# The front of the first expert layer in finer steps: three sequences by turns, inverse roots from logarithm and exponential, router products two token tiles at a time

## The chip, the cores and the metric

The kernel runs on one core of a Trainium2 chip, as one program. The metric is the device time of one execution in microseconds (us); the kernel before took 5645.84 us as the median of 3 runs (5634.86 to 5657.25). The engines are named as in the profile: PE is the matrix engine (TensorE; PEld is its weight load, which overlaps PE), DVE is VectorE, ACT is ScalarE, POOL is GpSimd, SP is the engine whose queue issues most of the DMAs.

## The reference

The network is two layers on x of shape (8, 1024, 256) in float32: eight sequences of 1024 tokens with 256 channels. Layer 0 is an expert layer, causal attention, and the same expert layer again; layer 1 is a channel mix, a state-space block and a channel mix. Every block works on the layer norm of x and is added to x. What matters here is the start of the first expert layer, which this document calls the front:

```python
def _layernorm(x, axis=-1, eps=1e-05):
    m = jnp.mean(x, axis=axis, keepdims=True)
    v = jnp.var(x, axis=axis, keepdims=True)
    return (x - m) / jnp.sqrt(v + eps)

# in _L0_ffn_ref, on xf = the layer norm of x, 8192 rows of 256
logits = xf @ Wr + br                 # 8 experts
Sm = jax.nn.softmax(logits, axis=-1)
G_t, idx_t = jax.lax.top_k(Sm.T, k)   # k = 8192 / 8 = 1024 tokens for each expert
...
x = x + 0.5 * _L0_ffn_ref(_layernorm(x, axis=-1), ...)
x = x + _L0_attn_ref(_layernorm(x, axis=-1), ...)
x = x + 0.5 * _L0_ffn_ref(_layernorm(x, axis=-1), ...)
```

For every token the front makes the normalised row, the eight logits and their softmax.

## The kernel before, in words

A sequence lies in on-chip memory as a tile `xt` of 128 partitions by 8 token tiles by 256 channels. `tile_macaron_kernel` loads all eight sequences by eight DMAs, runs the front over them, then picks the tokens of each expert (`moe.chosen`, which calls `choose`), then runs the experts (`moe.run`), then attention, then layer 1. `choose` needs the probabilities of all eight sequences, so the end of the front is a point that everything behind waits for.

The front is a Python generator, `Moe.steps_front`, whose `yield`s cut it into steps. The loop in `tile_macaron_kernel` holds up to two of these generators and gives each a step by turns; a new one may enter at every fourth turn. Inside `tc.manual_schedule()` each engine gets its instructions in the order in which the program issues them, so the turns fix every engine's queue; each engine works through its queue in that order and waits where an input is missing.

The steps of one sequence in `Moe.steps_front` are: `net.normalise` as one step (the statistics of the 8 token tiles, L75 and L77 on DVE; the square root on ACT, L79; the reciprocal on DVE, L81; eight subtract-and-scale operations on DVE, L88); then four steps with the transposes of two token tiles each (L180 on PE, 4 transposes; L184 copies the PSUM bank to `moe_xT` on ACT); then one step with all router products (L189: 16 matmuls in float32, which the trace shows as 32 records) and the addition of the bias (L194 on DVE); then the softmax, in which L203 is the exponential on ACT; then the write of the rows (`rows`, SP's queue) and of the probabilities (`S`, L213). After a sequence the loop writes `xt` to `acc` on SP's queue. The square root and the exponential are in different table sets of ACT, so a load of a table stands ahead of some of them.

The class `Attention` has its own version of the front, `Attention.steps_front`, which the kernel already uses for the second expert layer, one sequence at a time within attention (`store` calls it). It goes in finer steps: `Attention.stats` takes two token tiles a step, and gets the inverse root from ACT's logarithm and exponential (L619, L620) and one Newton step of four small POOL operations (L623 to L626), with one POOL operation ahead (L615). Two token tiles are normalised in one step (L876) and transposed in the next (L683, through `transposed`). The router products go two token tiles at a time (L890: 4 matmuls, 8 records), each pair with its own PSUM bank and its own bias addition (L894). Banks come from `bank`, and what empties a bank is held back in the object `Pipe` until the next bank is asked for, by whichever sequence asks.

Of the kernel before, what the change touches and what calls it, by code (L numbers as in the profile page):

```python
# [14 lines left out]
PSUM = bass.MemoryType.PSUM  # L15
# [1734 lines left out]
@with_exitstack  # L1750
def kernel(
    ctx: ExitStack,
    tc: tile.TileContext,
    x: bass.AP,
    w_qkv: bass.AP,
    w_out: bass.AP,
    b_out: bass.AP,
    Wr: bass.AP,
    br: bass.AP,
    W_up: bass.AP,  # L1760
    b_up: bass.AP,
    W_down: bass.AP,
    b_down: bass.AP,
    ln_gamma: bass.AP,
    ln_beta: bass.AP,
    in_proj_t: bass.AP,
    conv_w: bass.AP,
    conv_b: bass.AP,
    x_proj_t: bass.AP,
    dt_proj_t: bass.AP,  # L1770
    dt_proj_b: bass.AP,
    A_log: bass.AP,
    Dp: bass.AP,
    out_proj_t: bass.AP,
    Wr_t: bass.AP,
    Wk_t: bass.AP,
    Wv_t: bass.AP,
    mu_r: bass.AP,
    mu_k: bass.AP,
    out: bass.AP,  # L1780
):
    nc = tc.nc
    B, T, _ = x.shape
    net = Net(ctx, tc, B, T)
    N, NT = net.N, net.NT

    of_moe = ctx.enter_context(ExitStack())
    mcp = of_moe.enter_context(tc.tile_pool(name="moe", bufs=1, side="right"))
    moe = Moe(mcp, net, Wr, br, W_up, b_up, W_down, b_down)
    S = moe.probabilities(mcp)  # L1790
    dram1 = ctx.enter_context(tc.tile_pool(name="dram1", bufs=1, space=DRAM))
    dram2 = ctx.enter_context(tc.tile_pool(name="dram2", bufs=2, space=DRAM))

    acc = [dram1.tile([N, D], F32, name=f"acc{i}") for i in range(2)]
    rows = [dram1.tile([N, ROW], F32, name=f"rows{i}") for i in range(2)]

    def of(a, b):

        return a[b * T : (b + 1) * T, :].rearrange("(c p) d -> p c d", p=P)

    def pool_in(st, name, bufs, **kw):
        return st.enter_context(tc.tile_pool(name=name, bufs=bufs, **kw))

    xf, of_out = x.rearrange("b t d -> (b t) d"), out.rearrange("b t d -> (b t) d")
    with ExitStack() as st:
        at = Attention(net, pool_in(st, "at_w", 1), w_qkv, w_out, b_out)
        with ExitStack() as ro:
            room = moe.room(ro)
            with ExitStack() as ph, tc.manual_schedule():
                pool, px = pool_in(ph, "f", 2), pool_in(ph, "f_x", B)  # L1810
                ps = pool_in(ph, "f_ps", 3, space=PSUM)
                xs = []
                for b in range(B):
                    xs.append(px.tile([P, NT, D], F32, name="xt"))
                    nc.sync.dma_start(xs[b], of(xf, b))

                todo, works = list(range(B)), []
                turn = 0
                while todo or works:
                    if todo and len(works) < 2 and turn % 4 == 0:  # L1820
                        b = todo.pop(0)
                        works.append((b, moe.steps_front(pool, ps, xs[b], b, rows[0], S, "mm")))
                    turn += 1
                    for b, steps in list(works):
                        if next(steps, 0) == 0:
                            works.remove((b, steps))
                            nc.sync.dma_start(of(acc[0], b), xs[b])
            with tc.manual_schedule():
                moe.chosen(S, room)
        with tc.manual_schedule():  # L1830
            moe.run(S, rows[0], acc[0])
        with ExitStack() as ph:
            at.places(pool_in(ph, "at_qk", 1), dram1)
            pools = {
                name: pool_in(ph, f"at_{name}", bufs) for name, bufs in (
                    ("x", 3), ("xn", 2), ("xT", 1), ("side", 1), ("pT", 4), ("so", 2), ("oT", 2),
                    ("over", 2), ("sm", 2), ("junk", 1), ("r", 1), ("rT", 1),
                )
            }
            for name, banks in (("s1", 3), ("s2", 3), ("po", 1), ("mm", 1)):  # L1840
                pools[name] = pool_in(ph, f"at_{name}", banks, space=PSUM)

            pools["dram"] = dram2

            def load(xt, b):
                nc.sync.dma_start(xt, of(acc[0], b))

            def store(xt, b):
                nc.sync.dma_start(of(acc[1], b), xt)
                yield from at.steps_front(moe, xt, b, rows[1], S)  # L1850

            with tc.manual_schedule():
                at.run(pools, load, store)
    with ExitStack() as st:
        w = pool_in(st, "l1_w", 1)
        layer1 = Layer1(
            net, w, Wr_t, Wk_t, Wv_t, mu_r, mu_k, ln_gamma, ln_beta, in_proj_t, conv_w, conv_b,
            x_proj_t, dt_proj_t, dt_proj_b, A_log, Dp, out_proj_t,
        )
        with tc.manual_schedule():  # L1860
            with ExitStack() as ro:
                moe.chosen(S, moe.room(ro))
            moe.run(S, rows[1], acc[1])
        of_moe.close()
        pools = {
            name: pool_in(st, f"l1_{name}", bufs) for name, bufs in (
                ("x", 2), ("mixT", 1), ("ka", 2), ("r", 2), ("hT", 2), ("u", 1), ("uc", 2 * NDC),
                ("xd", 1), ("delta", 1), ("du", 1), ("sp1", 1), ("zs", 1),
                ("rep", 1), ("sdl", 3), ("sdu", 3), ("dbu", 2), ("hc", 6), ("tap", 1), ("through", 1), ("xn", 2), ("small", 2),
            )  # L1870
        }
        pools["dram"] = dram2
        pools["ps"] = pool_in(st, "l1_ps", 2, space=PSUM)
        pools["y"] = pool_in(st, "l1_y", 1, space=PSUM)
        pools["h"] = pool_in(st, "l1_h", 2, space=PSUM)

        def load(xt, b):
            nc.sync.dma_start(xt, of(acc[1], b))

        def store(xt, b):  # L1880
            nc.sync.dma_start(of(of_out, b), xt)

        def load_x(xt, b):
            nc.sync.dma_start(xt, of(acc[0], b))

        def keep_x(xt, b):
            nc.sync.dma_start(of(acc[0], b), xt)

        with tc.manual_schedule():
            layer1.run(pools, load, load_x, keep_x, store)  # L1890
# [39 lines left out]
```

## Time and profile before

| what | us |
|---|---|
| median of 3 runs (lowest, highest) | 5645.84 (5634.86, 5657.25) |
| the profiled execution's own time | 5638.44 |
| its span, first to last instruction | 5636.2 |
| start of the first statistics, end of the last copy to `S` | 12.20, 109.25 |
| `choose` and the list of the first experts behind it, to where PE fills up again | about 109 to 210 |
| mean granted clock of PE over the span | 0.888 |

The profile counts an engine as busy while it executes an instruction. "Idle before, releaser" gives the idle time of an engine ahead of an instruction, and what ended it. The clock column gives what share of the full clock PE was granted in a stretch. [...] Most of the front's stage lies in the first of the 40 slices of the page, so the stage is read from stretches cut by hand.

### The profile page before, as it was taken

The numbers are of one execution on the slowest core, as the hardware profiler recorded it, in microseconds if no ns is written. First come the engines' busy times: TensorE is split into PE (matmuls) and PEld (weight loads), VectorE is DVE, ScalarE is ACT, GpSimd is POOL, SyncE is SP. The second block draws the span as 40 slices with busy tenths as digits, with TensorE's granted clock in tenths as the row PEclk, the third lists the DMA queues.
The fourth block names the chain that finished last, engine by engine and source line by source line (L and its number), as shares of the span: only waits on it lengthen the run. The fifth ranks groups of instructions, "written<-read, shape, count | busy, mean of one in ns | idle before, by whom it ended". The sixth has DMA issues, their size and how long they took to land.

```text
span 5636.2 us, 60291 instructions
## 1 busy us (share of the span) xinstructions
PE 4643.4 (82%) x21302; PEld 2203.4 (39%) x21302; DVE 3432.4 (61%) x5653; ACT 2503.6 (44%) x4150; POOL 2204.0 (39%) x1801
## 2 busy tenths in 40 slices
PE   5699699999999997499776778787787878878767
PEld 5365334444444442265433233332333324333324
DVE  5532166667766672533108877777767677677884
ACT  2111155655556653011135546465564655646443
POOL 1234111111111110234317656556556565556662
PEclk6799789999999997599888889889898888989888
DMA  6132212212222221122215554535445463454642
GB/s 209 32 64 53 73 45 77 67 63 77 74 67 65 74 69 47 48 55 58 41 40 141 145 141 111 155 107 149 126 109 156 112 160 109 113 150 119 168 136 64
DMA packets 252976, 545.28 MB, mean 97 GB/s; under 512 B 29681, under 2 KB 143681, under 8 KB 252674
## 3 DMA queue, kind: packets, MB, share of 16 engines
q1 hardware_dynamic: 228098, 507.34, 32.0%
q0 software_dynamic: 24576, 34.10, 3.7%
q8 instruction: 168, 2.75, 0.2%
q14 instruction: 134, 1.10, 0.1%
HBM read 400.31 MB, written 141.03 MB: 96 GB/s over the span
## 4 chain that ended last, share of the span: by engine, by line
PE 26%; DVE 13%; ACT 6%; issue 5%; DMA 2%; POOL 1%; SPq 0%; DVEq 0%; POOLq 0%; ACTq 0%
DVE h L1729 8%; PE y L1657 5%; PE pc L1376 4%; PE pr L1271 4%; PE pk L1249 4%; PE pu L1427 2%; DVE hc L1734 2%; PE pp L1511 2%; ACT h L1635 2%; PE pd L1442 1%; PE pm L472 1%; ACT xn L1205 1%; PE px L1406 1%; DMA sdu<-du 1%; PE po L489 1%
## 5 line engine op out<-in xcount | busy, mean ns | idle before, releaser
L777 ACT ACTIVATE pT<-s 128x512 f32<-128x512 f32 (+3 forms) x1536 | 670.8, 488 | 554.4 <-PE s L734 545.0
L1635 ACT ACTIVATE h<-sdl,A 128x1024 f32<-128x1024 f32 x512 | 567.0, 1112 | 645.4 <-DVE hc L1734 623.7
L734 PE MATMUL s<-kT,qT 32*128 32x512 f32 (+3 forms) x3072 | 841.6, 541 | 12.6 <-DVE mx L750 7.9
L1657 PE MATMUL y<-hc,pick 128*32 128x512 f32 x2048 | 654.7, 720 | 227.7 <-DVE hc L1734 227.7
L734 PE MATMUL s<-qT,kT 32*128 32x512 f32 (+3 forms) x3072 | 763.8, 548 | 13.1 <-ACT pT L777 13.1
L1626 POOL TENSOR_TENSOR dbu<-sdu,b 128x1024 f32<-128x1024 f32 x256 | 602.2, 2352 | 407.3 <-DMA sdu<-du 209.7
L1729 DVE TENSOR_TENSOR_SCAN h<-h,dbu 128x1024 f32<-128x1024 f32 x256 | 586.1, 2289 | 185.6 <-ACT h L1635 159.7
L1729 DVE TENSOR_TENSOR_SCAN h<-h,sdu 128x1024 f32<-128x1024 f32 x256 | 586.1, 2290 | 158.1 <-ACT h L1635 140.7
L1734 DVE TENSOR_TENSOR hc<-h,c 128x1024 f32<-128x1024 f32 x512 | 625.3, 1221 | 32.2 <-PE y L1657 3.4
L783 POOL TENSOR_SCALAR_AFFINE_SELECT pT<-pT 128x512 f32<-128x512 f32 x256 | 162.4, 634 | 1180.2 <-ACT pT L777 1095.0
L1626 POOL TENSOR_TENSOR sdu<-sdu,b 128x1024 f32<-128x1024 f32 x256 | 602.4, 2353 | 15.3 <-DMA b<-bc 4.7
L734 PEld LDWEIGHTS s<-kT,qT 32*128 32x128 f32 x3072 | 327.0, 187 | 438.9 <-DVE mx L750 186.7
L476 ACT ACTIVATE mid<-pm,bu 128x512 f32<-128x512 f32 x192 | 131.6, 686 | 722.2 <-PE pm L472 722.2
L747 DVE TENSOR_REDUCE part<-s 128x1 f32<-128x512 f32 x512 | 329.5, 685 | 186.5 <-PE s L734 185.9
L1657 PEld LDWEIGHTS y<-hc,pick 128*32 128x32 f32 x2048 | 127.0, 125 | 717.4 <-issue 395.2
L497 POOL DMA_INDIRECT acc<-o,idx x128 | 208.5, 1629 | 492.6 <-DVE o L494 228.0
L750 DVE CUSTOM_DVE_ANT_0 junk<-s,mask,part 128x256 f32<-128x256 f32 (+3 forms) x512 | 281.5, 550 | 160.0 <-PE s L734 115.2
L472 PE MATMUL pm<-tT,wu 128*128 128x512 f32 x768 | 364.4, 612 | 0.0
L489 PE MATMUL po<-wd,mid 128*128 128x256 f32 x1536 | 346.1, 388 | 0.0
L797 PE MATMUL po<-pT,at_v 128*32 128x512 f32 (+3 forms) x3072 | 337.2, 512 | 0.3 <-POOL pT L783 0.3
L750 DVE CUSTOM_DVE_ANT_0 junk<-s,mask 128x256 f32<-128x256 f32 (+3 forms) x512 | 250.2, 489 | 142.7 <-PE s L734 90.1
L489 PEld LDWEIGHTS po<-wd,mid 128*128 128x128 f32 x1536 | 300.0, 196 | 43.3 <-issue 1.0
(262 smaller groups left out, 6696.1 us busy)
## 6 DMA issues: line engine op xcount, KB each, us to landing
sdl<-dl SPq DMA_DIRECT2D x256, 512.0 KB
sdu<-du SPq DMA_DIRECT2D x256, 512.0 KB
acc<-xt SPq DMA_DIRECT2D x24, 1024.0 KB
xt<-acc SPq DMA_DIRECT2D x24, 1024.0 KB
rows<-moe_r SPq DMA_DIRECT2D x16, 1056.0 KB
qT<-padded_q SPq DMA_DIRECT2D x32, 512.0 KB
kT<-padded_k SPq DMA_DIRECT2D x32, 512.0 KB
kept<-so SPq DMA_DIRECT2D x64, 256.0 KB
```

The lines of the kernel that those rows point to most:

```text
L472: nc.tensor.matmul(pm, wu[:, k, n * P : (n + 1) * P], tT[:, k, t0 : t0 + HALF], start=(k == 0), stop=(k == KC - 1),)
L489: nc.tensor.matmul(po, mid[:, n, j * P : (j + 1) * P], wd[:, n, :], start=(n == 0), stop=(n == NF - 1),)
L734: self.net.nc.tensor.matmul(s[:, 0 : rhs.shape[-1]], lhsT, rhs, start=True, stop=True)
L747: nc.vector.tensor_reduce(part, sh, AX.X, ALU.max)
L750: nc.vector.tensor_tensor_reduce(junk[:, 0:w], sh[:, 0:w], self.mask[:, W - w : W], 1.0, part if a else -3e38, ALU.add, ALU.max, self.mx[n ...
L777: self.net.nc.scalar.activation(pT[:, h, 0:w], sh[:, 0:w], AF.Exp, scale=1.0 / HD**0.5)
L797: nc.tensor.matmul(q.po[h * HS : (h + 1) * HS, o:W], self.va[q.b % 2][:, j, g * HG + h, :], pT[:, h, 0 : W - o], start=(j == 0), stop=(j = ...
L1626: nc.gpsimd.tensor_tensor(inputs[i], t, seqs[b].rep["b", p], ALU.mult)
L1635: nc.scalar.activation(decays[i], spread["dl", i - p], AF.Exp, scale=self.A[:, p, n : n + 1])
L1657: nc.tensor.matmul(self.py[g * self.RG : (g + 1) * self.RG, t0 : t0 + W], self.pick[:, j, :], hc[:, t0 : t0 + W], start=False, stop=(j == ...
L1729: nc.vector.tensor_tensor_scan(decays[i], decays[i], inputs.pop(i), 0.0, ALU.mult, ALU.add)
L1734: nc.vector.tensor_tensor(hc, decays.pop(i), seqs[b].rep["c", p], ALU.mult)
```

## The change

The loop in `tile_macaron_kernel` takes the generator from `Attention.steps_front` in place of the one from `Moe.steps_front`. It holds up to three sequences, and one may enter at every ninth turn. The pools are those that the new generator asks for: four buffers of each small tile, three of the row tile and of the transposed tile, four PSUM banks. ACT's table set with both the logarithm and the exponential is loaded once, ahead of the loop. The functions called (`Attention.stats`, `transposed`, `steps_front`, `bank`, `Pipe`) are unchanged, and nothing behind the loop is changed.

```diff
             with ExitStack() as ph, tc.manual_schedule():
-                pool, px = pool_in(ph, "f", 2), pool_in(ph, "f_x", B)
-                ps = pool_in(ph, "f_ps", 3, space=PSUM)
+                px = pool_in(ph, "f_x", B)
+                at.pools = {
+                    name: pool_in(ph, f"f_{name}", bufs) for name, bufs in (
+                        ("sm", 4), ("r", 3), ("rT", 3),
+                    )
+                }
+                at.pools["mm"] = pool_in(ph, "f_mm", 4, space=PSUM)
+                at.pipe = at.Pipe()
+                nc.scalar.preload_act_table_set("natural_log_exp_and_others")
                 xs = []
...
-                    if todo and len(works) < 2 and turn % 4 == 0:
+                    if todo and len(works) < 3 and turn % 9 == 0:
                         b = todo.pop(0)
-                        works.append((b, moe.steps_front(pool, ps, xs[b], b, rows[0], S, "mm")))
+                        works.append((b, at.steps_front(moe, xs[b], b, rows[0], S)))
```

The called generators, as they stand:

```python
def stats(self, x, got):                 # L600-627
    for c0 in range(0, NT, 2):
        yield ""
        for c in range(c0, c0 + 2):
            nc.vector.bn_stats(st[:, c, :], x[:, c, :])
        for c in range(c0, c0 + 2):
            nc.vector.bn_aggr(mv[:, c, :], st[:, c, :])
    yield ""
    nc.gpsimd.tensor_scalar(v, mv[:, :, 1], 1e-5, None, ALU.add)
    yield ""
    nc.scalar.activation(r, v, AF.Ln)
    nc.scalar.activation(r, r, AF.Exp, scale=-0.5)
    yield ""
    ...                                  # four POOL operations

def steps_front(self, moe, x, b, rows, S):   # L862-920
    yield from self.stats(x, got)
    for c0 in range(0, NT, 2):
        yield ""
        ...                              # L876, two token tiles
        yield "pe"
        self.transposed(r, c0, ...)      # 4 transposes, copy held back in Pipe
    for c0 in range(0, NT, 2):
        yield "pe"
        pl = self.bank([P, 2, E], "pl")
        ...                              # L890, 4 matmuls
        self.pipe.filled(...)            # L894, bias, held back in Pipe
    yield ""
    self.pipe.flush()
    ...                                  # maximum, difference
    yield ""
    nc.scalar.activation(lg, lg, AF.Exp)
    yield ""
    ...                                  # sum, reciprocal, product
    yield ""
    ...                                  # copy to S, DMA of the rows
```

## The prediction

> **What bounds the kernel now.** I read the page first. Its line of granted clocks begins at 6 tenths, so the first slice, where the change lies, is one in which PE is throttled. Then I cut the front's stage by pairs of sequences and read the busy time of the engines (columns: length, PE, PEld, DVE, ACT and POOL busy with instruction counts, PE's clock, DMA share, GB/s):
>
> ```profile
> 12.20:35.19 22.99, 15.05 (x96) 14.44 (x96) 15.01 (x65) 8.06 (x14) 0.00 (x0) 0.85 1.10 348
> 35.19:57.77 22.58, 14.75 (x96) 13.93 (x96) 15.00 (x65) 8.05 (x14) 0.00 (x0) 0.65 0.62 213
> 57.77:86.58 28.81, 20.96 (x96) 20.14 (x96) 15.11 (x66) 8.05 (x14) 0.00 (x0) 0.50 0.50 165
> 86.58:109.37 22.79, 14.75 (x96) 13.93 (x97) 15.09 (x65) 8.05 (x14) 0.00 (x0) 0.65 0.51 170
> ```
>
> The stage is 97 us, 1.7% of the span. A pair takes 22.6 to 28.8 us and keeps DVE busy 15 of them, so no engine is full; the clock decides between 22.8 and 28.8. The chain of waits, in order of time, shows why DVE stands still:
>
> ```profile
> 61.10 1.28 ACT L79 ACT_TABLE_LOAD   x1 [4.22 <-DVE ln_mv L77]
> 62.73 0.20 DVE L81 RECIPROCAL ln_rs<-ln_sd 128x8 f32<-128x8 f32 x1 [1.71 <-ACT ln_sd L79]
> 67.01 6.83 PE L189 MATMUL moe_pl<-wr,moe_xT 128*128 128x8 f32 x32
> 84.59 0.22 DVE L194 TENSOR_TENSOR moe_lg<-moe_pl,br 128x64 f32<-128x64 f32 x1 [6.58 <-PE moe_pl L189]
> ```
>
> DVE waits for PE's router products (6.58 us at that place) and for a root behind a table load. At full clock the same 32 products took 3.73 us (at 21.44 us). Then PE's clock in stretches of 3.4 us. The first two lines count the transposes alone (length, PE, PEld and ACT busy, clock, DMA), the others all of PE (length, PE busy, clock, DMA):
>
> ```profile
> 41.98:45.40 3.42, 2.65 (x13) 2.25 (x11) 2.34 (x4) 0.50 0.53 187
> 72.60:76.00 3.40, 2.30 (x10) 2.24 (x11) 0.59 (x1) 0.50 0.00 0
> ...
> 45.43:48.80 3.37, 3.37 (x32) 1.00 0.00 0
> 69.20:72.60 3.40, 3.40 (x17) 0.50 0.01 2
> ```
>
> Each spell at full clock but the first lasts 3.4 us. One began after the stretch at 41.98, with 2.65 us of transposes; none after the one at 72.60, with 2.30 us, nor after the one at 69.20, which is router products without a gap. The full-clock stretch of products at 45.43 was followed by 0.50. So transposes, packed closely, raise the clock; router products don't, and don't hold it. Last, the new code, as it already runs by itself at the end of attention, at clock 0.50:
>
> ```profile
> 2247.04 0.24 POOL L615 TENSOR_SCALAR ln_v<-ln_mv 128x8 f32<-128x8 f32 x1 [3.01 <-DVE ln_mv L612]
> 2250.20 2.67 DVE L876 TENSOR_SCALAR moe_r<-xt,ln_mv,ln_r 128x256 f32<-128x256 f32 x8 [2.62 <-POOL ln_r L626]
> 2250.76 1.13 PE L683 MATMUL tr<-ident,moe_r 128*128 128x128 f32 x4 [8.86 <-DVE moe_r L876]
> 2257.95 1.87 PE L890 MATMUL pl<-wr,moe_xT 128*128 128x8 f32 x8 [0.68 <-ACT moe_xT L881]
> 2260.09 1.87 PE L890 MATMUL pl<-wr,moe_xT 128*128 128x8 f32 x8 [0.27 <-DVE moe_lg L894]
> ```
>
> It gives every step of the new front its duration.
>
> **The change, part by part.**
>
> *Table loads.* Eight loads of 1.283 us leave ACT (four before the root, four before the exponential), 10.3 us, all ahead of something waited for. This is a gain, contained in the walk below.
>
> *Root.* From the last statistics to the first scaling, before: 61.02 to 62.97, 1.95 us with its load. After: POOL, ACT twice, POOL four times; the alone-run has 3.16 us from 2247.04 to 2250.20, less one load 1.28, so 1.88 us. Once, at the start, two POOL memsets (0.51 and 0.30) have slid behind L615 and delay the root by 0.2. SP's DMAs are the same sixteen in the same order; none is waited for (a sequence's buffers come back three sequences later).
>
> *Statistics.* A pair of tiles now takes 0.86 us on DVE (2243.55 to 2244.41), four pairs 3.44, against 2.71 + 0.62 = 3.33. Nothing to speak of.
>
> *The order on DVE and PE.* The built queues repeat every nine turns. With sequence B in the middle, A ending, C new, DVE's cycle is: last scaling of B; first bias of B; first scaling of C; second and third bias of B; second scaling of C; then statistics of the next sequence with the rest between. PE's is: last transposes of B, products 1, 2, 3 of B, first transposes of C, products 4 of B, then C's transposes. DVE therefore asks for B's products right after scaling what PE must first transpose. At clock 0.50: scaling a pair 0.68 on DVE; from its start to the end of its transposes 1.69 (2250.20 to 2251.89), PE free at 1.43; a group of products 1.87, the next one 1.71 behind it (6.83/32 x 8). From the last scaling at 0:
>
> - products 1 end at 3.30, first bias 3.34 to 3.55: DVE has idled 2.66; C's first scaling, whose root is ready at 1.8, to 4.23
> - products 2 end at 5.01, bias at 5.05: idle 0.82, to 5.25
> - products 3 end at 6.72, bias at 6.76: idle 1.50, to 6.97; scaling and statistics to 8.51
> - C's transposes take PE to 7.42, products 4 end at 9.29, bias at 9.33: idle 0.82; maximum and difference to 10.04
> - statistics 0.86, scaling 0.68, statistics 0.86, softmax 0.74 (its exponential long done), statistics 0.86, copy 0.20: 14.24
>
> The cycle is 14.24 us: 8.43 work and 5.80 waiting. At full clock (0.93 a group, PE free at 1.22) the same walk leaves 1.66 + 0.06 + 0.76 of waiting, 10.9 us. Before, a sequence took 11.3 to 11.5, and 14.4 in the throttled pair.
>
> *Which clock.* In the cycle PE's transposes come in four groups of 1.13, from 6.6, 9.1, 11.5 and 14.8 us: 3.4 us hold at most 2.2 us of them (9.2 to 12.6), less than the 2.30 that raised nothing. So I take 0.50, with at most the first cycle at full clock. This is the choice that decides; both ends are kept.
>
> [...]
>
> *Sum.* Statistics from 12.20, root to 17.9, then 5.48 of scalings and statistics to the first last-scaling at 23.4. Six cycles; a seventh without new statistics (11.7 at 0.50, 7.9 warm); the last sequence's products and softmax (10.5, 7.2 warm).
> - 0.50: 23.4 + 85.4 + 11.7 + 10.5 = 131.0 against 109.25: +21.8; up to 3.4 less if the first cycle is warm: I take +21.
> - warm: 23.4 + 65.4 + 7.9 + 7.2 = 103.9: -5.
>
> *Behind the front.* `choose` begins with the last copy to `S`, and from 109 to 210 us it is one chain of DVE and PE, with the expert weights loaded from 117 to 126 us and used after 200: the shift passes on whole. The work behind is identical. The profiled time 5638.4 becomes 5659; it lies 7.4 below the median of the runs, so the median becomes 5667.
>
> **Rivals.**
>
> 1. *The clock holds at full.* For it: it stood at 1.00 from the start to 24.75 us, also over DVE-paced transposes. Against: every later full stretch of products ended in 0.50. 5646 - 5 = 5641. Decided by whether it outlives the second cycle.
> 2. *Slower by over 0.5%: each group on PE begins only once the one before has drained.* The alone-run has 2.14 from group to group where 1.71 is the packed slot. 0.43 more at four places of each cycle is 1.7, over six cycles and the tail +13: 5680. It decides from 0.22 us exposed per group, where +28 is passed. For it: PE's queue has an extra semaphore instruction ahead of each group of transposes. Against: in the alone-run one bank forces it, here there are four, and PE's waits on itself go back three groups or more.
> 3. *It does what it looks like: all waits of DVE are covered.* 8.43 a cycle: 23.4 + 50.6 + 5.0 + 7.2 = 86.2, -23: 5623. Against: DVE's first bias stands directly behind the scaling that it depends on through PE.
>
> **How the numbers follow.** Forecast 0.66, rival 1 0.10, rival 2 0.19, rival 3 0.05. Runs of the kernel before differ by 11 either way, and 0.5% of it, 28 us, is about what a measurement can tell from no change. The forecast's +21 with that spread passes 28 one time in four, giving 0.17; rival 2 gives nearly all its 0.19; so slower 0.36. Faster by 28 needs rival 3 and luck: 0.02. The rest, 0.62, is within 0.5%. The range reaches from just above rival 1 (5645) to rival 2 with its spread (5690).
>
> **What would show it.** Right: the stage ends near 131 us; clock 0.50 from 25 us on; about 14.2 from one sequence's copy to `S` to the next; DVE's idle time is put to L890, some 5 to 6 us a cycle; no table loads. Wrong: full clock after 30 us; a cycle under 11.5; idle time ahead of L876 put to POOL; groups of L890 more than 1.9 us apart though queued.

## The result and the profile after

The changed kernel takes 5664.78 us (median of 12 runs), against 5648.66 us for the kernel before (12 runs taken beside them): a ratio of 1.003, with a 95% interval of 1.0016 to 1.0043. It is slower by 16 us, within half a per cent. One of the twelve runs took 6474.09 us at a granted clock of 0.706, where the others had 0.899 to 0.903; without it the median is 5664.77. The prediction was 5667.

The profiled execution of the changed kernel took 5683.01 us, 18 above its own median, so only its early part is compared here. The front ends (the last copy to `S`) at 126.56 us, where it ended at 109.25 before: +17.3. The experts' first product at L472 starts at 226.56 instead of 209.26, again +17.3, so the shift passes on whole. What lies behind the front's end is the same code in both kernels and in every experiment below, and took between 5529 and 5556 us in the nine profiled executions (profiled time less the front's end), in no order that goes with the front; that scatter is not a finding about the change.

The stretches of the front, from the trace after (columns: length, PE, PEld, DVE, ACT and POOL busy with instruction counts, PE's clock, DMA share, GB/s). The first three are two sequences each, the last is the end:

```profile
23.23:50.49 27.26, 21.28 (x96) 19.39 (x96) 15.62 (x69) 5.97 (x14) 2.31 (x10) 1.00 0.59 192
50.49:77.77 27.28, 21.18 (x96) 19.37 (x96) 15.65 (x70) 5.97 (x14) 2.41 (x10) 1.00 0.46 157
77.77:105.05 27.28, 21.17 (x96) 19.38 (x96) 15.65 (x71) 5.97 (x14) 2.41 (x10) 1.00 0.47 157
105.05:126.66 21.61, 18.35 (x84) 17.30 (x84) 7.19 (x32) 3.83 (x9) 1.21 (x5) 1.00 0.58 198
```

A pair of sequences takes 27.3 us each time, where it took 22.6 to 28.8 before. DVE is still busy 15.6 of them; PE is now busy 21.2, where it was 14.75 in the quicker pairs before. The clock column reads 1.00, and that must not be believed here (see below). What DVE waited for in the front, before and then after (engine, output and line that waited, what it waited for: us in total, times, longest):

```profile
DVE moe_lg L194 <- PE moe_pl L189: 19.2, 5, 6.6
DVE ln_rs L81 <- ACT ln_sd L79: 8.5, 8, 1.7
DVE moe_sm L206 <- ACT moe_lg L203: 7.5, 8, 2.5
```

```profile
DVE moe_lg L894 <- PE pl L890: 47.7, 32, 2.5
DVE moe_r L876 <- POOL ln_r L626: 2.0, 1, 2.0
DVE moe_sm L908 <- ACT moe_lg L905: 0.3, 1, 0.3
```

The change did what its edits say: the waits for the root and for the exponential fall from 16.0 us to 2.3. But the wait for the router products grows from 19.2 to 47.7, in 32 places where there were 5. All waits together are 35.2 before and 50.0 after, +14.8; DVE's own busy time over the front is 60.2 before and 63.0 after, +2.8. That accounts for the 17.3. One cycle of DVE, from its timeline (start, length, instruction, and in brackets the idle time just before it and what ended it):

```profile
36.85 0.73 DVE L876 TENSOR_SCALAR moe_r<-xt,ln_mv,ln_r 128x256 f32<-128x256 f32 x2
40.08 0.17 DVE L894 TENSOR_TENSOR moe_lg<-pl,br 128x16 f32<-128x16 f32 x1 [2.51 <-PE pl L890]
41.79 0.18 DVE L894 TENSOR_TENSOR moe_lg<-pl,br 128x16 f32<-128x16 f32 x1 [0.89 <-PE pl L890]
43.50 0.17 DVE L894 TENSOR_TENSOR moe_lg<-pl,br 128x16 f32<-128x16 f32 x1 [1.53 <-PE pl L890]
45.95 0.17 DVE L894 TENSOR_TENSOR moe_lg<-pl,br 128x16 f32<-128x16 f32 x1 [0.76 <-PE pl L890]
...
50.49 0.73 DVE L876 TENSOR_SCALAR moe_r<-xt,ln_mv,ln_r 128x256 f32<-128x256 f32 x2
```

The four biases start at 40.08, 41.79, 43.50 and 45.95: the first three 1.71 apart, which is one group of eight products (products are counted here as the trace has them, two records to a matmul). PE's side of it:

```profile
37.40 1.14 PE L683 MATMUL tr<-ident,moe_r 128*128 128x128 f32 x4 [1.94 <-DVE moe_r L876]
38.33 5.13 PE L890 MATMUL pl<-wr,moe_xT 128*128 128x8 f32 x24
```

Twenty-four products without a gap take 5.13 us, 0.213 us each. Before, 32 of them took 6.83 us (0.213 each) in a stretch marked 0.50, and 3.73 us (0.117 each) in one marked 1.00. So PE ran the changed front at half clock throughout. All 256 products, from the groups by line (busy us, mean ns of one, and the idle time before them), before and after:

```profile
L189 PE MATMUL moe_pl<-wr,moe_xT 128*128 128x8 f32 x256 | 37.8, 289 | 0.4 <-ACT moe_xT L184 0.2
```

```profile
L890 PE MATMUL pl<-wr,moe_xT 128*128 128x8 f32 x256 | 54.7, 353 | 0.0
```

The same 256 products keep PE busy for 54.7 us where they took 37.8.

### The profile page after: what moved, and what is told of

Read it like the earlier page. It is cut to its first block, busy times and chain, and to the rows that moved or that the text cites. A ratio compares the mean times of both kernels' runs of the same rounds, so it can differ in the third digit from the quotient of the medians.

```text
span 5681.1 us, 60336 instructions
## 1 busy us (share of the span) xinstructions
PE 4683.4 (82%) x21302; PEld 2229.9 (39%) x21302; DVE 3436.1 (60%) x5669; ACT 2496.2 (44%) x4150; POOL 2218.6 (39%) x1841
## 3 DMA queue, kind: packets, MB, share of 16 engines
q1 hardware_dynamic: 228098, 507.34, 31.9%
## 4 chain that ended last, share of the span: by engine, by line
PE 26%; DVE 13%; ACT 6%; issue 5%; DMA 2%; POOL 1%; SPq 0%; DVEq 0%; POOLq 0%; ACTq 0%
DVE h L1729 8%; PE y L1657 5%; PE pc L1376 4%; PE pr L1271 4%; PE pk L1249 4%; PE pu L1427 2%; DVE hc L1734 2%; PE pp L1511 2%; ACT h L1635 2%; PE pd L1442 1%; PE po L489 1%; ACT xn L1205 1%; PE px L1406 1%; PE pm L472 1%; DMA sdu<-du 1%
## 5 line engine op out<-in xcount | busy, mean ns | idle before, releaser
L734 PE MATMUL s<-qT,kT 32*128 32x512 f32 (+3 forms) x3072 | 767.6, 550 | 12.9 <-ACT pT L777 12.8
L472 PE MATMUL pm<-tT,wu 128*128 128x512 f32 x768 | 363.9, 611 | 0.0
```

The source lines that it names most:

```text
L472: nc.tensor.matmul(pm, wu[:, k, n * P : (n + 1) * P], tT[:, k, t0 : t0 + HALF], start=(k == 0), stop=(k == KC - 1),)
L734: self.net.nc.tensor.matmul(s[:, 0 : rhs.shape[-1]], lhsT, rhs, start=True, stop=True)
```

## The experiments

The theory has two parts. The first: in the new order DVE asks for a sequence's first products straight after the scaling that PE must still transpose, and then for each further group as fast as PE makes them, so DVE idles 5 to 6 us a cycle. The second: those products are paid at half clock, because matmuls of 8 columns neither raise PE's clock nor hold it. The rivals: the new roots on POOL, or the number of sequences in work, are what costs; or the order costs, whatever the clock.

### Router products of 128 columns

The changed kernel with the eight columns of `Wr` repeated sixteen times, so that each product streams 128 columns; the bias reads the first eight.

```diff
+        self.wide = cp.tile([P, KC, P], F32, name="wide")
+        nc.vector.tensor_copy(
+            self.wide.rearrange("p k (r e) -> p k r e", e=E),
+            self.wr.unsqueeze(2).to_broadcast([P, KC, P // E, E]),
+        )
...
-            pl = self.bank([P, 2, E], "pl")
+            pl = self.bank([P, 2, wr.shape[-1]], "pl")
...
-                        pl[:, c, :], xT[...], moe.wr[:, k, :],
+                        pl[:, c, :], xT[...], wr[:, k, :],
```

> The changed kernel with one edit: each router product of the front streams 128 columns (the eight of Wr sixteen times over) in place of 8; the extra columns are read by nobody. [...] Theory (router products do not count as work for the clock, columns streamed do): PE now streams without a gap for 9.5 us of each cycle, the clock rises, groups of products come under 1.2 us apart for most of the stage, the cycle falls from 13.64 to 10.3 to 12 us and the stage ends at 103 to 116 us instead of 126.7. Rival (the slow products are a matter of records and queues, not of the clock): groups stay 1.71 us apart, the stage ends at 126 us or later.

The front ended at 111.7 us, 14.9 earlier than in the changed kernel, with sixteen times the columns to stream. Cycles were 11.4 and 12.5 us by turns. The median was 5656.95 us, a ratio of 1.0001 (0.9987 to 1.0016) to the kernel before. One cycle on PE, from its timeline:

```profile
61.19 3.78 PE L896 MATMUL pl<-wide,moe_xT 128*128 128x128 f32 x24
64.80 0.60 PE L688 MATMUL tr<-ident,moe_r 128*128 128x128 f32 x4
65.24 1.06 PE L896 MATMUL pl<-wide,moe_xT 128*128 128x128 f32 x8
```

Twenty-four products begin at half clock and end at full (the column reads 0.58 from 60.3 to 63.7 us and 1.00 from there to 67.1): 3.78 us where the 8-column ones took 5.13; the eight behind them took 1.06. This is the second part of the theory. The rival, that the slow products are a matter of records and queues and the end stays at 126 or later, falls. DVE's wait for products is 33.2 us in all, 14.5 less than in the changed kernel, which is nearly all of the gain.

### Products asked for three turns later

The changed kernel with three empty turns between a sequence's transposes and its products.

```diff
+        for _ in range(gap):      # gap=3
+            yield ""
         lg = pools["sm"].tile([P, NT, E], F32, name="moe_lg")
```

> The changed kernel with three empty turns between a sequence's last transposes and its router products, so that DVE's first bias no longer stands directly behind the scaling that it depends on through PE. The clock should stay throttled. Theory (DVE waits because of the order of its own queue): the 2.5 us wait ahead of the first bias falls to about 1.1, the cycle from 13.64 to about 12.0, the stage ends near 116 us. Rival (PE is simply the bound at half clock, 10.3 us of slots and its drains): the wait moves to another bias and the cycle stays within 0.3 of 13.64, the end within 3 us of 126.7.

The front ended at 119.3 us, 7.3 earlier than in the changed kernel, with cycles of 12.31 us. The median was 5662.64 us, a ratio of 1.0023 (1.0008 to 1.0038).

```profile
40.95 0.17 DVE L896 TENSOR_TENSOR moe_lg<-pl,br 128x16 f32<-128x16 f32 x1 [0.98 <-PE pl L892]
42.66 0.17 DVE L896 TENSOR_TENSOR moe_lg<-pl,br 128x16 f32<-128x16 f32 x1 [1.53 <-PE pl L892]
```

The wait ahead of the first bias falls from 2.51 to 0.98 us, as the first part of the theory has it. The gain is smaller than expected (a cycle of about 12.0 and an end near 116 us): the groups are still 1.71 us apart, so the next bias waits 1.53, and a short wait for the root comes in (0.3 us a cycle). At half clock the order alone doesn't pay for the change.

### Both

```diff
-                        works.append((b, at.steps_front(moe, xs[b], b, rows[0], S)))
+                        works.append((b, at.steps_front(moe, xs[b], b, rows[0], S, moe.wide, 3)))
```

> Both edits: 128 columns streamed, and three empty turns ahead of the products. Theory: with the clock up and the order mended DVE's work alone sets the cycle, 8.0 to 9.5 us, and the stage ends at 88 to 98 us, ahead of the 109.3 of the kernel before by 11 to 21 us, so 0.2 to 0.4% faster than it. Rival (the clock does not rise): the same end as with the empty turns alone. Rival (order alone counts): the end lies no more than 3 us ahead of that.

The front ended at 102.2 us, 7.1 before the kernel before; the cycle was 10.24 to 10.37 us. The median was 5642.63 us, a ratio of 0.9979 (0.9965 to 0.9993). Together the two edits gain 24.4 us on the changed kernel, a little more than their sum alone (14.9 and 7.3), but the size was missed: 88 to 98 was expected. The clock is the likely cause again, and the next run tests it. PE and its clock in two neighbouring stretches (columns as above):

```profile
44.55:47.96 3.41, 1.73 (x12) 1.31 (x13) 3.03 (x12) 1.29 (x5) 0.85 (x5) 1.00 0.33 113
47.96:51.37 3.41, 3.41 (x19) 3.41 (x18) 1.32 (x7) 0.45 (x1) 0.00 (x0) 0.50 1.04 348
```

The clock is lost at 47.96, after 3.41 us in which PE was busy for 1.73, and comes back at 51.37, after 3.41 us without a gap. So the first two groups of every cycle run at half clock (sixteen products in 3.33 us at 57.88, 0.208 each, nearly the slot of the 8-column ones), and one wait of 1.53 stays.

### Both, with PE kept busy

The version above with twelve transposes of the identity behind each sequence's third and fourth pair of transposes, into a bank of their own that nobody reads. If the lost clock is the cause of the miss, it must go.

```diff
+        if more:                  # 12 behind the third and fourth pair
+            junk = self.pools["warm"].tile([P, P], F32, name="warm")
+            for _ in range(more):
+                self.net.nc.tensor.transpose(junk, self.net.ident, self.net.ident)
         self.pipe.filled(lambda: take(pt))
```

> The variant with 128 columns and three empty turns, and 12 idle transposes of the identity after the third and after the fourth pair of transposes of each sequence, where PE stood idle; nobody reads what they write. Theory (the clock of that variant fell for 3.4 us in each 10.25 us cycle because PE streamed too little there, and its 1.5 us wait ahead of a bias lay in those spells): the clock stays up, the cycle falls to 8.6 to 9.4 us and the stage ends at 92 to 98 us instead of 102.3. Rival (the extra work is in the way of the products): the end is 102 us or later.

The front ended at 94.2 us, the cycle was 8.89 us, and the clock, once up, stayed up: the column reads 1.00 from 36.5 to 70.5 us, and the last groups of products still lie 0.89 us apart (84.27 and 85.16). The median was 5640.17 us, a ratio of 0.9965 (0.9953 to 0.9977): quicker than both kernels, by doing more work on PE.

```profile
61.29 1.47 PE L695 MATMUL warm<-ident 128*128 128x128 f32 x12
...
63.17 1.95 PE L902 MATMUL pl<-wide,moe_xT 128*128 128x128 f32 x16
```

Sixteen products now take 1.95 us, 0.12 each. Of DVE's waits in a cycle two are left, one for the products and 0.27 us for the root on POOL:

```profile
56.27 0.17 DVE L906 TENSOR_TENSOR moe_lg<-pl,br 128x16 f32<-128x16 f32 x1 [0.72 <-PE pl L902]
```

### Two sequences instead of three

The changed kernel with two sequences in work, one entering at every twelfth turn.

```diff
-                    if todo and len(works) < 3 and turn % 9 == 0:
+                    if todo and len(works) < 2 and turn % 12 == 0:
```

> The changed kernel with two sequences by turns, a new one at every twelfth turn, in place of three at every ninth. The clock stays throttled. Theory (what counts is what DVE has in its queue between the last scaling and the first bias): with this order three steps of statistics lie between them, the cycle is 12.9 us instead of 13.64 and the stage ends at 118 to 123 us. Rival (three sequences cover more waiting than two): the cycle is longer than 13.64 and the stage ends after 127 us.

The front ended at 112.0 us, 14.6 earlier than with three sequences, and earlier than expected. The cycle is 12.48 us, and one of them is 9.6, around a spell at full clock (43.4 to 46.6 us) that came by itself. Of the 14.6 us, 8.1 are there at the first copy to `S` (28.68 us, where it came at 36.77). There the groups of products are 0.89 us apart, so the clock was up in the first sequence too, against what was expected:

```profile
25.26 0.17 DVE L894 TENSOR_TENSOR moe_lg<-pl,br 128x16 f32<-128x16 f32 x1 [0.72 <-PE pl L890]
26.16 0.17 DVE L894 TENSOR_TENSOR moe_lg<-pl,br 128x16 f32<-128x16 f32 x1 [0.72 <-PE pl L890]
```

How much of the 8.1 is that clock and how much the start with two sequences was not separated. What compares the two orders is the regular cycle. The median was 5655.96 us, a ratio of 0.9988 (0.9977 to 0.9999); by the front alone it should be 2.7 us slower than before, which lies 3.3 us above the interval's upper end; that is not explained. In the regular cycle of this order the first bias waits for nothing, and the other three for a group each:

```profile
55.61 0.17 DVE L894 TENSOR_TENSOR moe_lg<-pl,br 128x16 f32<-128x16 f32 x1
57.31 0.17 DVE L894 TENSOR_TENSOR moe_lg<-pl,br 128x16 f32<-128x16 f32 x1 [1.53 <-PE pl L890]
59.02 0.17 DVE L894 TENSOR_TENSOR moe_lg<-pl,br 128x16 f32<-128x16 f32 x1 [1.53 <-PE pl L890]
60.73 0.17 DVE L894 TENSOR_TENSOR moe_lg<-pl,br 128x16 f32<-128x16 f32 x1 [1.53 <-PE pl L890]
```

So a third sequence in work doesn't by itself cover the waits. Nor does it cost by itself: the run with three empty turns has three sequences and a cycle of 12.31 us. What counts in the cycle is where a sequence's products stand in DVE's queue.

The regular cycles of five versions can now be laid side by side, each as the waits of one cycle and the rest, from DVE's waits between two copies to `S`:

| version | cycle, us | waits in it, us | rest, us |
|---|---|---|---|
| changed kernel | 13.64 | 5.69 (products) | 7.95 |
| two sequences | 12.48 | 4.6 (products) | 7.9 |
| three turns later | 12.31 | 4.0 (products) + 0.3 (root) | 8.0 |
| 128 columns, later | 10.27 | 2.1 (products) + 0.3 (root) | 7.9 |
| the same, PE kept busy | 8.89 | 0.72 (products) + 0.27 (root) | 7.90 |

DVE's own work is 7.9 to 8.0 us a sequence in every one of them, and what the cycles differ by is DVE's waits, nearly all of them for PE.

### The new roots alone

The kernel before, with its own order and its own products, but with the root from logarithm, exponential and a Newton step on POOL, its table set loaded once ahead of the loop as in the changed kernel (one load in the trace there, 1.28 us at 0.81, and none in the front).

```diff
-        net.normalise(pool, r, x, net.eps5)
+        ...
+        nc.gpsimd.tensor_scalar(v, mv[:, :, 1], 1e-5, None, ALU.add)
+        nc.scalar.activation(rs, v, AF.Ln)
+        nc.scalar.activation(rs, rs, AF.Exp, scale=-0.5)
+        ...                       # four POOL operations, then the scaling
```

> The kernel before with one part of the change alone: the inverse roots from logarithm and exponential with the Newton step on POOL, so that the eight table loads are gone; steps, turns and products as before. Theory (the loads are worth little, since the root by way of POOL takes 1.9 us, as long as the square root with its load): the stage ends within 4 us of 109.3. Rival (the loads are the gain that the change was to bring, 1.28 us on each of eight waits): the stage ends near 99 us.

The front ended at 111.2 us, 2.0 later than before; the median was 5660.76 us, a ratio of 1.0012 (0.9997 to 1.0027). Nothing is gained (DVE's waits, columns as above):

```profile
DVE moe_lg L214 <- PE moe_pl L209: 19.8, 5, 7.6
DVE moe_r L190 <- POOL ln_r L188: 15.8, 8, 2.0
DVE moe_sm L226 <- ACT moe_lg L223: 3.3, 8, 1.0
```

The exponential is waited for 4.2 us less in all (3.3 for 7.5), but the root is waited for 7.3 us more (15.8 for 8.5). In the kernel before only every second root stands behind a table load, and DVE waits 1.71 us for it; for the four others it waits 0.37 to 0.43 us:

```profile
69.23 0.20 DVE L81 RECIPROCAL ln_rs<-ln_sd 128x8 f32<-128x8 f32 x1 [0.43 <-ACT ln_sd L79]
```

The new root, two ACT and five POOL operations one behind the other, is waited for 1.97 to 2.03 us every time: a little more than a square root with its load, and 1.5 us more than one without. The changed kernel has the same root and waits for it once (2.0 us), because its statistics run a sequence ahead. The root was made harmless by the order, not by itself, and it isn't what made the changed kernel slower.

### The kernel before with products of 128 columns

```diff
-        pl = ps.tile([P, NT, E], F32, name="moe_pl", tag=tag)
...
+        for c0 in range(0, NT, 4):
+            pl = ps.tile([P, 4, P], F32, name="moe_pl", tag=tag)
...
-                    pl[:, c, :], xT[...], self.wr[:, k, :],
+                        pl[:, c, :], xT[...], self.wide[:, k, :],
```

> The kernel before (old steps, square roots, two sequences) with its router products streaming 128 columns, eight of which are read; the products then lie in two PSUM banks and their bias is added in two operations. Theory (the clock is what the old front loses in its throttled pair, and what its products lose elsewhere): no pair takes the 28.8 us that one took, all four take 20 to 23 us, and the stage ends at 94 to 104 us instead of 109.3. Rival (the old front is held by its coarse steps alone): the end stays within 4 us of 109.3.

The front ended at 101.5 us, 7.75 earlier than before, and all four pairs took 21.7 to 22.9 us; the slow pair of 28.8 is gone. The median was 5646.64 us, a ratio of 0.998 (0.9968 to 0.9991). DVE's wait for the products is now short and regular, 12.9 us in all where it was 19.2:

```profile
DVE moe_lg L203 <- PE moe_pl L198: 12.9, 8, 1.6
```

So this one edit gains 7.75 us in the old order, where the whole change lost 17.3. It also cuts the products and their bias in two, and what that part is worth alone was not measured; that the 256 products keep PE busy for 31.9 us, where they took 37.8, speaks for the clock.

## Why the prediction was right, point by point

**Order on DVE and PE: right, and the waits nearly to the figure.** The walk gave 2.66, 0.82, 1.50 and 0.82 us ahead of the four biases; they measured 2.51, 0.89, 1.53 and 0.76, together 5.69 for 5.80. The experiment with three empty turns shows that the first of them depends on the distance in DVE's queue from the last scaling to the first bias.

**The term that was mis-sized is DVE's work in the cycle**: 8.43 us predicted, 7.95 measured. The walk let every instruction begin when the one before had ended. In the trace, instructions that don't depend on each other overlap: the bias at 40.08 takes 0.17, and the scaling behind it begins at 40.17, not at 40.25. Over six cycles this is 2.9 us, and the waits 0.7.

**Sum**: 23.4 + 85.4 + 11.7 + 10.5 = 131.0 was predicted for the half clock; measured are 23.2, 81.8 (six cycles of 13.64), 11.2 and 10.3, together 126.5. The allowance of up to 3.4 for a first cycle at full clock wasn't needed: the first cycle measures 13.62, like the others. The front's shift of +17.3 stands for the +21 that was taken, and the medians differ by 16.1. The median alone would hardly have told the mechanism: the sums for half and full clock (131.0 and 103.9) lie 27 us apart, half a per cent of the kernel, so it is the front's own times that bear it out.

**Which clock: right in the choice and in its reason.** The products' slot is 0.213 us from the first cycle to the last, and the transposes were never packed as closely as the 2.65 us in 3.4 that stood ahead of a rise of the clock before; the closest were 2.48 us, from 18.4 to 21.8. The widened products show directly that the columns streamed count: with 128 columns the clock rises within the 24 products, and with groups of twelve idle transposes more it stays up, once it has risen, to the last products of the front.

With matmuls of 128 columns the clock came back after 3.41 us of PE work without a gap (the stretch at 47.96). Products of 8 columns without a gap for 5.13 us (at 38.33 in the changed kernel) did not bring it up, and a stretch with PE busy for 1.73 of 3.41 us, far from idle, was followed by its loss (the stretch at 44.55).

**What would show it** named a clock column of 0.50 from 25 us on. That was wrong: the column reads 1.00, and by the sign "full clock after 30 us" it would have spoken against the choice of clock. The two other signs, 13.64 between copies to `S` (14.2 predicted) and 5 to 6 us of idle time a cycle put to L890, decided it, with the slots.

**Table loads and root**: the prediction calls the 10.3 us of table loads that leave ACT a gain, contained in the walk. Its comparison of the roots (1.95 us before, 1.88 after) holds for a root with a load only; half of the old roots have none and are waited for about 0.4 us. Taken alone, the new root with no loads makes the front 2.0 us longer. In the changed kernel this didn't matter. The root was waited for once, 2.0 us (1.88 and 0.2 for the memsets were predicted).

**Rival 1**, the clock holding at full by itself, did not come about, and what spoke for it rested in part on the column of the kernel before, which reads too high at the start (see the last section); what a held clock is worth in exactly this order was not isolated, since the run that held it also moved the products. **Rival 2**, groups drained one by one, is false: the groups are 1.71 us apart, not 2.14. **Rival 3**, all waits covered, was false for this order, but its price was real: with the products later, wider and the clock held, the cycle is 8.89 us, 1 us above DVE's work.

**Behind the front**: L472 shifts by the front's 17.3 us exactly, as predicted.

## What to carry to other kernels

When a stage is cut finer, write down for each engine which instruction its queue stands on (here DVE's on a first bias, for 2.51 us), and how long ago the work that it needs was started: here a third stream covered little, because the waiting instruction came straight behind the one that feeds it. Before trusting PE's speed in a stage of small matmuls, look at how many columns they stream: narrow ones may stay at half clock even without a gap between them (here 8 columns, for 5.13 us), and repeating the columns, or adding matmuls that nobody reads, can make the stage quicker (here 14.9 us, and 8.0 more on top of the later products). A stall removed on one engine (a table load) is a gain only if what replaces it ends earlier where it is waited for.

## What the runs showed that was not expected

The clock column can mislead. In the changed kernel it reads 1.00 in every stretch from the start to 305 us, with the first fall there, though the products' slots in the front are those of half clock (0.213 us, against 0.12 with the clock up). The kernel before shows the same at its start. The column reads 1.00 there from the first us to 24.75, but the first sixteen transposes take as long as sixteen at 63.52 us, where it reads 0.50:

```profile
17.96 3.69 PE L180 MATMUL tr_moe<-ident,moe_r 128*128 128x128 f32 x16 [17.96 <-DVE moe_r L88]
63.52 3.69 PE L180 MATMUL tr_moe<-ident,moe_r 128*128 128x128 f32 x16 [7.77 <-DVE moe_r L88]
```

The products behind them, from 21.44 us, have the slots of full clock (32 in 3.73 us). By this reading the first spell at full clock, too, lasted about 3.3 us, from 21.44 to 24.75, and closely packed transposes stood ahead of it. The slot of a known matmul is the surer sign.

The spells are regular: in the run with 128 columns and later products the clock is up for 6.8 us and down for 3.4, cycle after cycle. The front's cycle of 10.24 to 10.37 us lies close to that period; whether one sets the other was not tested. What in PE's work raises the clock or keeps it, and what a matmul of 8 columns adds to that, stays open: these runs only show 8 columns on one side and 128 on the other.
